# A spectral token-mixer kernel: modes loaded four blocks ahead in the last output, more tiles for the inverse transforms, and the sum x1 + lam y written for all blocks

## The chip, the cores and the metric

The kernel runs on one core of one Trainium2 chip. All data are float32. The metric is the device time of one launch, in microseconds (us); smaller is better. The profile is one execution of the same program with the hardware profiler on.

## The reference, cut to what matters

The input is 256 rows of 256 x 128 values. Layer 0 is a gated attention along the rows, added to its input; its result is called x1. Layer 1 sees x1 as 256 tokens (a token is an image of 256 x 128 pixels), lets the tokens attend to each other through a few Fourier modes of each image, and then mixes the tokens in groups of four with two Fourier layers. The diff touches only layer 1. Its end is this:

```python
attn = fno_layer(attn, p_wr, p_wi, p_bias, p_sw, p_sb, (H, W))
attn = instance_norm(attn + tokens, attn_norm_w, attn_norm_b)
attn = attn.reshape(b * (C // TOKEN_CODIM), TOKEN_CODIM, H, W)
h0 = instance_norm(attn, norm2_w, norm2_b)
h1 = fno_layer(h0, mix_wr[0], mix_wi[0], mix_bias[0], mix_sw[0], mix_sb[0], (H, W), norm=True, act=True)
h2 = fno_layer(h1, mix_wr[1], mix_wi[1], mix_bias[1], mix_sw[1], mix_sb[1], (H, W), norm=True)
out = instance_norm(h2, mon_w, mon_b) + attn        # and x1 is added to out by the caller

# fno_layer(x): skip = einsum(x, sw);  spec = irfft2(keep_low_modes(rfft2(x)) * w) + bias
#               y = (instance_norm(spec) if norm else spec) + skip;  gelu(y) if act
```

`instance_norm` takes mean and variance over the pixels of an image. The kernel writes the image before the mixer (attn + tokens, not yet normed) as y. The normed image is lam y plus a constant, so the final result is x1 + lam y + kap h2 + c0, with one lam, kap and c0 for each token.

## The kernel before, in words

**Halves, blocks, pixels.** The 256 tokens are cut into two halves of 128, `a` = 0 and 1; a token of the half is a partition. The 32768 pixels of an image are cut into 16 blocks of NB = 2048 pixels (b), each of two half blocks of HB = 1024 pixels (u or k in the code, 0 to 31). A tile of one half block is 128 x 1024 values, 512 KB; one of a block is 1 MB. All 16 blocks of one half stay in SBUF as `blocks` (`hb[b]` is one block), 16 MB; that is why other tiles are few.

**Fourier modes.** An image is kept as 32 x 16 modes. Turning modes into pixels takes two matmul steps. The first, `synth_modes` (lines 540 to 590), goes along the image's height: matmuls with `esyn` into four PSUM banks, four copies into a tile `gt` (128 x 2048 values, two by ACT and two by DVE, line 581), and four writes of a quarter each to a DRAM tensor `Gd` (line 586). It is called for one quarter of the modes at a time (`chunk` c = 0 to 3). The second, `image`, is done block by block: `load_modes` reads the modes of a block into a tile `gs` by four loads of 64 KB (lines 1199 and 1204), and 32 small matmuls (line 1182) add the image to PSUM. `skip` (line 1193) adds the channel product of four tokens to the same banks. Modes with a weight other than one are handled by a scaled copy `esyn0` of the first 32 rows of esyn, used for c = 0 and f = 0.

**Stages of layer 1.** They begin after some 1650 us; layer 0 is what comes before.
1. To about 1900 us: modes of x1, the attention between tokens (matrix `mpT`), and the modes of its result, written to `Gd0`.
2. `y_blocks(0)`, to about 2050 us: y of half 0. For each half block two tiles of x1 (one `xt` tile, line 997), 16 matmuls with mpT (line 1317), `image` from Gd0, four products by DVE (line 1327) into `blocks`, and statistics (line 1329). The first two blocks (b < NW = 2) are also written to the DRAM tensor `yd`. Before this stage a few small constants are loaded (ch4, sel4, s4, lines 1230 to 1255).
3. `y_blocks(1)`, half blocks 0 to 23, to about 2200 us: the same for half 1, all of it written to yd, woven with `first_modes(0)`, which computes the norm of y, the mixer's first product of modes (`mix_modes`) and the writes of `Gd1` of half 0.
4. `first_images(0)`, 2200 to 2345 us: for each block `skip` and `image` of Gd1 into `ups`, Gelu by ACT (line 1483) back into `blocks`, then, one block behind, 16 transposes (`htps`, line 1490), four copies `hT` (three by DVE, line 1502, one by ACT, line 1493), `skip` again for the statistics of the second layer (line 1510) and a forward transform (psA, yA, lines 1513 to 1516) into `Yd`. In the same loop, `load_w` and `add_w` (lines 1459 to 1470) make w = x1 + lam y for blocks 2 to 15: load x1 into half of an `xw` tile, lam y by ACT, the add by GpSimd (POOL), and a write to the DRAM tensor `wd`. This must come before Gelu overwrites y in `blocks`.
5. To about 2404 us: half blocks 24 to 31 of `y_blocks(1)`, woven with the start of `second_modes(0)`, which reads Yd back (tile `YT`, line 1534) and transforms it along the height (`f1ps`, line 1551).
6. 2404 to 2545 us: `mix_modes` of second_modes(0) (names z0) and of first_modes(1) (x1), their synth_modes (g20 into `Gd2` of half 0, g11 into `Gd1` of half 1), and blocks 0 to 4 of `output_0`. For blocks 0 and 1, `output_0` loads y and x1 and adds them itself (line 1637); for the others it loads w.
7. 2545 to 2716 us: `first_images(1)`, woven with blocks 5 to 15 of `output_0`.
8. 2716 to 2801 us: `second_modes(1)`, woven with `Output1.ahead`, which loads y and x of five half blocks (lines 1659 and 1661) and lets DVE make x1 + lam y in place (line 1666).
9. 2801 us to the end: `Output1.run`. For each block: `output` (lines 1594 to 1609), which does skip and image of Gd2 into `h2ps`, four ACT passes kap h2 + c0 (line 1602), two DVE adds to w (line 1608) and two writes by POOL's queue (line 1609); then the modes of block b + 2, DVE's add for further half blocks, and loads of y and x of half blocks 2b + 9 and 2b + 10.

**What sets the order.** From stage 2 on the order of instructions of each engine, SP included, is the order of the program text (`manual_schedule`). Python generators are woven by hand: `weave` advances a side generator when a running sum of written costs is positive. So SP issues its loads strictly one after another, and a load that waits for its tile holds all that follow. A tile's wait comes from its pool: `tile(tag, bufs=n)` gives the same memory again after n calls, and the first use then waits for the last use of the tile before. Loads go through SP; the writes of wd, yd, Yd, Gd1, Gd2 and of the result go through POOL's queue. DMA issues of SP and of ACT also take turns on eight semaphores: an issue waits until the DMA eight turns back has landed.

**Pools that matter here.** `xp` holds xt (3 tiles of 1 MB), gs (2) and yt (2). output_0 takes its tiles from the same tags until 2545 us. Output1 has two pools: `self.wp`, which lives from stage 8, and `more`, which opens at 2801 us. Before, half blocks k with k % 9 < 5 use `wp` (5 x tiles, 2 y tiles) and the others `more` (4 x tiles, 2 y tiles).

Of the kernel before, what the change touches and what calls it, by code (L numbers as in the profile page):

```python
# [10 lines left out]
FP = mybir.dt.float32  # L11
# [7 lines left out]
P = 128  # L19
# [493 lines left out]
def layer1(tc, I, C, ident, x1d, upool, U, stats2, mv2, out):  # L513
# [9 lines left out]
    with ExitStack() as ctx:  # L523
# [16 lines left out]
        def synth_modes(pool, psum, Z, T, Gd, tag, spare=None, turned=False, chunk=None, ptag="s", gbufs=2, queue=None):  # L540
# [4 lines left out]
            for c in range(4) if chunk is None else (chunk,):  # L545
                for part in range(1 if both else 2):
                    ps = [psum.tile([P, 512], FP, tag=ptag, name=f"{tag}gp_{c}_{part}_{f}") for f in range(4)]
                    gt = pool.tile([P, 4, 512], FP, tag="gt", name=f"{tag}gt_{c}_{part}", bufs=gbufs)
                    for ri in range(2) if both else (part,):
                        for jp in range(2):  # L550
                            k = 2 * ri + jp if both else jp
                            for i in range(2):
                                for f in range(4):
                                    q = slice(32 * f, 32 * f + 32)
                                    e = esyn0 if c == 0 and f == 0 else esyn
                                    trig = (1 - i if ri else 2 * i)
                                    if spare is not None and c == 0 and f == 0 and ri == 1:
                                        if i == 0:
                                            nc.tensor.matmul(
                                                ps[f][:, k * T : (k + 1) * T], e[0:32, 0, jp * P : (jp + 1) * P],  # L560
                                                spare, start=True, stop=True,
                                            )
                                    elif not turned:
                                        nc.tensor.matmul(
                                            ps[f][:, k * T : (k + 1) * T], e[q, trig, jp * P : (jp + 1) * P],
                                            Z[q, c, i, :], start=(i == 0), stop=(i == 1),
                                        )
                                    else:
                                        for jj in range(2):
# [7 lines left out]
                                                e[q, trig, j * 64 : (j + 1) * 64],  # L577
# [4 lines left out]
                    for ri in range(2) if both else (part,):  # L582
                        for jp in range(2):
                            k = 2 * ri + jp if both else jp
                            r0 = 16 * ri + 4 * c
                            (queue or nc.sync).dma_start(  # L586
# [58 lines left out]
        with tc.manual_schedule(engines=COMPUTE):  # L645
# [316 lines left out]
            esyn0 = late.tile([32, 3, H], FP, name="esyn0")  # L962
# [21 lines left out]
            nc.vector.tensor_scalar(esyn0, esyn[0:32], wsyn[0:32, 0:1], None, ALU.mult)  # L984
# [15 lines left out]
        xts = {(0, u): load_x1(0, u) for u in range(3)}  # L1000

# [90 lines left out]
        with tc.manual_schedule(engines=COMPUTE):  # L1092
# [46 lines left out]
            values(7, 1)  # L1139
            for c in range(4):  # L1140
                synth_modes(wp, psg0, Z, NT, Gd0, "g0", spare=m1, chunk=c)
                if c < 2:
                    values(7, c + 2)
# [21 lines left out]
        NW, NX = 2, 5  # L1165
# [59 lines left out]
        with tc.tile_pool(name="psb", bufs=4, space=PSUM) as psa, tc.tile_pool(name="spb", bufs=1) as spb:  # L1225
            same4 = load_const(spb, "same4")
            sel4 = load_const(spb, "sel4")

            ch4 = spb.tile([4, 6], FP, name="ch4")
            for i, src in enumerate(  # L1230
                (L("norm2_w"), L("norm2_b"), L("mix_sb")[0], L("mix_sb")[1], L("mon_w"), L("mon_b"))
            ):
                nc.sync.dma_start(ch4[:, i : i + 1], src.unsqueeze(1))
# [4 lines left out]
            an = sp.tile([P, 2], FP, name="an")  # L1238
            nc.sync.dma_start(an[:, 0:1], L("attn_norm_w").partition_broadcast(P))
            nc.sync.dma_start(an[:, 1:2], L("attn_norm_b").partition_broadcast(P))  # L1240

            blk = []
            for l in range(2):
                s4 = spb.tile([4, 4], FP, name=f"s4_{l}")
                with nc.allow_non_contiguous_dma(reason="16 elements"):
                    nc.sync.dma_start(s4, L("mix_sw")[l].rearrange("o i -> i o"))
                ps = psa.tile([P, 512], FP, tag="a", name=f"blkps_{l}")
                nc.tensor.matmul(ps[:, 0:4], sel4, s4, start=True, stop=True)
                r4 = spb.tile([P, 4], FP, name=f"r4_{l}")
                nc.vector.tensor_copy(r4, ps[:, 0:4])  # L1250
                bl = sp.tile([P, 32, 4], FP, name=f"blk_{l}")
                nc.vector.tensor_tensor(
                    bl, bc(r4, 1, 32), same4.rearrange("p (g o) -> p g o", o=4), ALU.mult
# [6 lines left out]
            nc.vector.tensor_scalar(hw0, wsyn[:, 1:2], 0.5, None, ALU.mult)  # L1260
# [660 lines left out]
```

## Time and profile before

Three runs gave 3015.53, 3019.59 and 3023.93 us; the median is 3019.59 us. The profiled execution has a span of 3018.5 us.

| engine | busy us | share of the span | instructions |
|---|---|---|---|
| PE (TensorE matmul) | 2621.3 | 87% | 28526 |
| PEld (weight load) | 1904.2 | 63% | 28526 |
| DVE (VectorE) | 2003.7 | 66% | 3223 |
| ACT (ScalarE) | 1467.7 | 49% | 2856 |
| POOL (GpSimd) | 1662.5 | 55% | 1310 |

Durations of single instructions that are needed below, in ns (mean of the group on the page or in an answer of the trace):

| line, engine | what | mean |
|---|---|---|
| L1327 DVE | y, one quarter of a half block, 128x256 | 418 |
| L1502 DVE / L1493 ACT | hT copy, 128x512 | 684 / 604 |
| L1510 DVE | statistics, 128x512 | 688 |
| L1466 ACT | lam y, 128x1024 | 1150 |
| L1469 POOL | x1 + lam y, 128x1024 | 2363 |
| L1666 DVE | x1 + lam y, 128x1024 | 1279 |
| L1608 DVE | w + blocks, 128x1024 | 1223 |
| L586 POOL | issue of one Gd write | 752 to 757 |
| L1609 POOL | issue of one result write | 535 |

How to read the page: busy time is the time in which an engine executes, and an engine that waits is not busy. A group's line gives the idle time just before its instructions and who ended it. The share of busy time is an average over stages with different limits, so the stage must be looked at by itself. "DMA" is the mean busy share of the core's 16 DMA engines, and "PEclk" the clock that TensorE was granted, as a share of full speed. SPq is the sequencer of SP, which issues loads; a wait there holds every later load.

### The profile page before, as it was taken

How to read it: one execution, taken by the hardware profiler on the slowest of the kernel's cores; microseconds unless marked ns; L12 is line 12 of the kernel's file. 1: busy time of each engine (PE TensorE's matmuls, PEld its weight loads, DVE VectorE, ACT ScalarE, POOL GpSimd, SP SyncE). 2: the span in 40 equal slices, each digit the busy share in tenths (PEclk: the TensorE clock that was granted, in tenths of full speed). 3: DMA queues.
4: the chain of work that ended last, by engine and by line, in shares of the span. 5: the costliest groups of instructions: out<-in, count | busy, mean ns of one | idle time of the engine just before them, and what ended most of it. 6: DMA issues, size and time to landing. Idle time of an engine off the chain costs nothing. (4 is left out here: it accounts for less than half of the span.)

```text
span 3018.5 us, 70144 instructions
## 1 busy us (share of the span) xinstructions
PE 2621.3 (87%) x28526; PEld 1904.2 (63%) x28526; DVE 2003.7 (66%) x3223; ACT 1467.7 (49%) x2856; POOL 1662.5 (55%) x1310
## 2 busy tenths in 40 slices
PE   6899999999999999999999899898998775886333
PEld 6677777777777777777776567686754543443111
DVE  7788888878888888888888447466555452563323
ACT  0477777777777777777776223000055013450212
POOL 0499999999999999999998002000257012111100
PEclk9999999999999999999999899999999887997555
DMA  9422222222222122222221012787878728974755
GB/s 364 154 66 65 71 66 66 65 73 66 64 72 66 66 65 72 66 64 72 65 66 47 19 50 78 255 274 267 309 259 299 258 77 292 323 264 150 260 213 210
DMA packets 226907, 430.02 MB, mean 142 GB/s; under 512 B 26070, under 2 KB 153513, under 8 KB 218520
## 3 DMA queue, kind: packets, MB, share of 16 engines
q1 hardware_dynamic: 200472, 333.24, 32.8%
q0 software_dynamic: 26112, 92.29, 8.6%
q8 instruction: 226, 3.70, 0.5%
q14 instruction: 97, 0.79, 0.1%
HBM read 290.17 MB, written 135.27 MB: 141 GB/s over the span
## 5 line engine op out<-in xcount | busy, mean ns | idle before, releaser
L299 POOL TENSOR_TENSOR e<-e,b1T 128x1024 f32<-128x1024 f32 x256 | 606.6, 2369 | 164.9 <-PE u L348 89.4
L303 POOL TENSOR_TENSOR es<-e 128x512 f32<-128x512 f32 x512 | 639.7, 1271 | 20.1
L281 ACT ACTIVATE sc<-sc,b2T 128x512 f32<-128x512 f32 x512 | 339.0, 662 | 365.0 <-PE sc L272 356.8
L323 DVE RECIPROCAL av<-av 128x256 f32<-128x256 f32 x256 | 452.3, 1767 | 27.2 <-DVE og L322 1.4
L281 ACT ACTIVATE e<-sc,b2T 128x512 f32<-128x512 f32 x512 | 348.6, 681 | 0.0
L294 DVE TENSOR_TENSOR e<-sc,b1T 128x1024 f32<-128x1024 f32 x256 | 311.0, 1215 | 0.0
L272 PE MATMUL sc<-qkT 32*128 32x256 f32 x4096 | 294.1, 401 | 1.3 <-DVE e L294 1.3
L311 PE MATMUL av<-e,v 128*32 128x256 f32 x4096 | 274.7, 385 | 0.5 <-POOL e L299 0.5
L1317 PE MATMUL yps<-xt,mpT 128*128 128x256 f32 x1024 | 245.9, 394 | 20.5 <-DMA xt<-x1d 10.4
L272 PEld LDWEIGHTS sc<-qkT 32*128 32x128 f32 x4096 | 185.6, 184 | 112.4 <-issue 97.8
L322 DVE SCALAR_TENSOR_TENSOR og<-gate,av 128x256 f32<-128x256 f32 x256 | 107.8, 421 | 190.6 <-PE av L316 190.6
L1317 PEld LDWEIGHTS yps<-xt,mpT 128*128 128x128 f32 x1024 | 195.1, 195 | 59.0 <-issue 10.9
L1182 PE MATMUL h2ps<-k_bsyn,gs 32*128 32x128 f32 x1024 | 65.0, 362 | 159.4 <-DMA gs<-Gd 159.4
L1602 ACT ACTIVATE blocks<-h2ps,col 128x512 f32<-128x512 f32 x128 | 89.2, 777 | 209.7 <-PE h2ps L1182 209.7
L327 POOL TENSOR_TENSOR x<-xt,bo 128x256 f32<-128x256 f32 x256 | 187.8, 734 | 0.0
L1182 PEld LDWEIGHTS h2ps<-k_bsyn,gs 32*128 32x128 f32 x1024 | 56.8, 253 | 201.1 <-DMA gs<-Gd 178.1
L246 PE MATMUL qk<-xnT,wT_wq 128*128 128x256 f32 x512 | 179.5, 432 | 1.7 <-ACT xnT L238 1.7
L1331 POOL DMA_DIRECT2D yd<-yt x32 | 17.3, 539 | 291.6 <-DVE yt L1327 291.6
L252 PEld LDWEIGHTS gv<-wT_wv,kvT 128*128 128x128 f32 x1024 | 155.0, 192 | 13.4
L316 PE MATMUL av<-es,ones 128*32 128x256 f32 x2048 | 157.5, 379 | 2.6 <-POOL es L303 2.5
L333 PE MATMUL wo<-wT_wo,og 128*128 128x128 f32 x1024 | 156.8, 276 | 2.7 <-DVE og L324 2.7
L348 PE MATMUL u<-adft,x 128*128 128x129 f32 x1024 | 156.4, 275 | 0.0
(532 smaller groups left out, 5347.3 us busy)
## 6 DMA issues: line engine op xcount, KB each, us to landing
xt<-x1d SPq DMA_DIRECT2D x128, 512.0 KB
xb<-in_x_dram SPq DMA_DIRECT2D x32, 1024.0 KB
xt<-in_x_dram SPq DMA_DIRECT2D x128, 256.0 KB
kt<-in_L_conv_kv_x_dram SPq DMA_DIRECT2D x128, 256.0 KB
x1d<-x SPq DMA_DIRECT2D x256, 128.0 KB
gs<-Gd SPq DMA_DIRECT2D x384, 64.0 KB
yd<-yt POOLq DMA_DIRECT2D x32, 512.0 KB, 5.5
y<-yd SPq DMA_DIRECT2D x16, 1024.0 KB
```

Source lines behind the costliest of these rows:

```text
L246: nc.tensor.matmul(ps[:, 0:256], wT["wq"], xnT, start=True, stop=True)
L272: nc.tensor.matmul(sc[h // 2][:, h % 2, c * 256 : (c + 1) * 256], qkT[p, 256 + c * P : 256 + (c + 1) * P], qkT[p, 0:256], start=True, stop ...
L281: nc.scalar.activation(r["e"][1][:, :, c, :] if hp else z, z, AF.Exp, bias=b2T[:, c, s : s + 1])
L294: nc.vector.tensor_tensor(r["e"][0].rearrange("p h c q -> p (h c q)"), r.pop("sc").rearrange("p h x -> p (h x)"), b1T[:, 0:2].rearrange("p ...
L299: nc.gpsimd.tensor_tensor(e1, e1, b1T[:, 2:4].rearrange("p h c q -> p (h c q)"), ALU.mult)
L303: nc.gpsimd.tensor_tensor(r["es"][hp], e[:, :, 0, :], e[:, :, 1, :], ALU.add)
L311: nc.tensor.matmul(ps[hd, 0:256], r["v"][:, c, hd], r["e"][h // 2][:, h % 2, c, :], start=(c == 0), stop=(c == 1),)
L316: nc.tensor.matmul(ps[32 * h : 32 * h + 32, 256:512], self.ones, r["es"][h // 2][:, h % 2, :], start=True, stop=True,)
L323: nc.vector.reciprocal(rd, rd)
L327: nc.gpsimd.tensor_tensor(r["x1"], r["x"], bc(self.bo, 1, 2), ALU.add)
L333: nc.tensor.matmul(ps[:, j * P : (j + 1) * P], r["og"][:, j * P : (j + 1) * P], wT["wo"], start=True, stop=True,)
L1317: nc.tensor.matmul(rows_of(ps[j]), mpT[:, sc, tt], by_turn(xt[:, sc])[:, j], start=(sc == 0), stop=False,)
```

## The change

The change has six parts.

1. **Output1**: `gs` gets four tiles (two in `wp`, two in `more`) and modes are loaded four blocks ahead. y has five tiles in turn (2 and 3), x has eight (5 and 3). Loads run for half blocks 2b + 8 and 2b + 9, and DVE's adds go up to half block 2b + 5.
2. **second_modes(1)**: two YT loads are issued at once, the others as tiles come free, and `ahead` starts only after the forward transform, with a cost of 0.4 for each step in place of 0.3.
3. **Inverse transforms**: `synth_modes` takes a list of pools for `gt`. g20 uses the three `xt` tiles, g11 takes its own tile and the xt tiles in turn. Of the four writes of a chunk, two are issued by POOL and two by ACT.
4. **w for all blocks**: `load_w` and `add_w` also run for blocks 0 and 1, so that output_0 has one form and y of half 0 is not written to yd. add_w of block b + 1 moves to just behind Gelu of block b. output_0 loads one block ahead, and its first load comes before the g11 chunks. In first_images(0) all four hT copies go to DVE.
5. **Small constants** (same4, sel4, ch4, an, s4) are loaded before the attention between tokens, and the two products with s4 become one.
6. **Weights of modes**: `esyn0` goes. The modes Z themselves are scaled in their first 32 rows (a separate tile Z0 in front of Gd0), and hw0 is divided by the weight again. `gs` in xp has three tiles in place of two.

The diff, cut to its core:

```diff
@@ synth_modes
-                    gt = pool.tile([P, 4, 512], FP, tag="gt", name=f"{tag}gt_{c}_{part}", bufs=gbufs)
+                    gp, gtag, gbufs = gts[c % len(gts)] if gts else (pool, "gt", 2)
+                    gt = gp.tile([P, 4, 512], FP, tag=gtag, name=f"{tag}gt_{c}_{part}", bufs=gbufs)
...
-                            (queue or nc.sync).dma_start(
+                            (queues or (nc.sync, nc.sync))[jp].dma_start(
@@ after xts, before the attention between tokens
+        par = _Held(tc.tile_pool(name="spb", bufs=1))
+        same4 = load_const(par.pool, "same4")
+        sel4 = load_const(par.pool, "sel4")
...
+            Z0 = sp.tile([32, 2, NT], FP, name="Z0")
+            nc.vector.tensor_scalar(Z0, Z[0:32, 0], wsyn[0:32, 0:1], None, ALU.mult)
@@ y_blocks
-                    gs[u // 2] = xp.tile([P, 4, P], FP, tag="gs", name=f"gs_{a}_{u}")
+                    gs[u // 2] = xp.tile([P, 4, P], FP, tag="gs", name=f"gs_{a}_{u}", bufs=3)
...
-                if a or b < NW:
+                if a:
                     nc.gpsimd.dma_start(ydv[:, a, u * HB : (u + 1) * HB], yt)
@@ mix_modes
+            nc.vector.tensor_scalar(Z[0:32, 0], Z[0:32, 0], wsyn[0:32, 0:1], None, ALU.mult)
@@ first_images
             load(0)
+            if a == 0:
+                load_w(0)
+                add_w(0)
...
-                    if a == 0 and b + 1 >= NW:
+                    if a == 0:
                         load_w(b + 1)
...
                         nc.scalar.activation(by_turn(hb[b])[:, j], rows_of(ps[j]), AF.Gelu)
+                    if a == 0 and b < 15:
+                        add_w(b + 1)
...
-                            nc.scalar.copy(t, ps)
+                            (nc.scalar.copy if a else nc.vector.tensor_copy)(t, ps)
...
-                if a == 0 and NW <= b + 1 < 16:
-                    add_w(b + 1)
@@ second_modes
             load(0)
             yield 6.0
+            if gbufs > 1:
+                load(1)
             for c in range(4):
-                if gbufs > 1 and c < 3:
-                    load(c + 1)
...
-                if gbufs == 1 and c < 3:
-                    load(c + 1)
+                if c + gbufs < 4:
+                    load(c + gbufs)
                     yield 4.0
@@ output_0
-                if b < NW:
-                    got[b] = [xp.tile([P, 2, HB], FP, tag="xt", name=f"xy_{b}_{s}", bufs=3) for s in range(2)]
...
+            load(0)
+            yield
             for b in range(16):
                 if b not in got:
                     load(b)
+                if b < 15 and pools[3]:
+                    load(b + 1)
@@ Output1.load
-                more = k % (NX + 4) >= NX
-                wp = self.more if more else self.wp
-                y = wp.tile([P, HB], FP, tag="yo", name=f"y4_{k}", bufs=2)
+                old = k < 5 or k % 5 < 2
+                y = (self.wp if old else self.more).tile(
+                    [P, HB], FP, tag="yo", name=f"y4_{k}", bufs=2 if old else 3
+                )
                 nc.sync.dma_start(y, ydv[:, 1, px])
-                x = wp.tile([P, HB], FP, tag="xo", name=f"x4_{k}", bufs=4 if more else NX)
+                x = (self.wp if k % 8 < 5 else self.more).tile(
+                    [P, HB], FP, tag="xo", name=f"x4_{k}", bufs=5 if k % 8 < 5 else 3
+                )
@@ Output1.run
-                    gs[b] = self.wp.tile([P, 4, P], FP, tag="gs", name=f"gs3_1_{b}")
+                    gs[b] = (self.wp if b % 4 < 2 else self.more).tile(
+                        [P, 4, P], FP, tag="gs", name=f"gs3_1_{b}", bufs=2
+                    )
...
-                for k in range(NX, NX + 4):
+                for k in (5, 6, 7):
                     self.load(k)
+                modes(2)
+                modes(3)
                 for b in range(16):
                     run(output(1, b, gs.pop(b), [self.w.pop(2 * b), self.w.pop(2 * b + 1)], psk))
-                    if b < 14:
-                        modes(b + 2)
+                    if b < 12:
+                        modes(b + 4)
                     for k in sorted(self.ld):
-                        if k < 2 * b + 4 or k < NX + 2 * b:
+                        if k <= 2 * b + 5:
                             self.add(k)
-                    for k in (2 * b + NX + 4, 2 * b + NX + 5):
+                    for k in (2 * b + 8, 2 * b + 9):
                         if k < 32:
                             self.load(k)
@@ the weaving
-                    m0 = second_modes(0, wp, tiles(wp), bq)
+                    m0 = second_modes(0, wp, tiles(wp), bq, [(xp, "xt", 3)])
...
+                    m1 = first_modes(
+                        1, wp, Tiles(F=(xp, "yt", 2), f=(xp, "yt", 2), m=(xp, "gs", 3)), br,
+                        [(wp, "gt", 1), (xp, "xt", 3)],
+                    )
...
                     o0 = output_0(pools, bq)
+                    next(o0)
...
-                    m1 = second_modes(1, wp, tiles(wp), Banks(psq, "q"), gbufs=2)
-                    weave((0.3 for _ in m1), o1.ahead())
+                    m1 = second_modes(1, wp, tiles(wp), Banks(psq, "q"), [(wp, "gt", 2)], gbufs=2)
+                    run(iter(lambda: next(m1), None))
+                    weave((0.4 for _ in m1), o1.ahead())
```

## The prediction, made before the changed kernel ran

> **What bounds the kernel now.** The slices of the page show two kernels in one. Up to about 1650 us (layer 0) PE is busy throughout and DMA at two tenths; the diff does not touch that. From 1900 us on DMA moves 200 to 300 GB/s and PE, its clock and DMA all sag at the end. So I cut this second part into its stages and asked for busy times of each (columns: stretch; length; PE, PEld, DVE, ACT, POOL busy with counts; granted clock; DMA share; GB/s):
>
> ```profile
> 2182.00:2192.00 10.00, 9.01 (x67) 7.21 (x66) 5.66 (x13) 0.00 (x0) 1.18 (x3) 1.00 1.03 376
> 2202.00:2345.00 143.00, 122.64 (x1896) 62.37 (x1892) 74.79 (x120) 80.81 (x124) 94.98 (x74) 1.00 0.84 282
> 2404.00:2447.00 43.00, 33.54 (x80) 14.89 (x80) 30.79 (x69) 3.35 (x7) 0.53 (x1) 0.88 0.19 67
> 2447.00:2482.00 35.00, 19.64 (x300) 16.21 (x300) 11.51 (x26) 5.75 (x12) 11.96 (x16) 0.78 0.42 116
> 2482.00:2545.00 63.00, 32.35 (x832) 21.78 (x832) 24.23 (x38) 19.71 (x30) 17.50 (x26) 0.69 0.78 273
> 2545.00:2716.00 171.00, 147.27 (x2624) 79.51 (x2624) 94.19 (x134) 81.08 (x140) 23.34 (x37) 0.92 0.88 297
> 2716.00:2748.00 32.00, 12.31 (x256) 9.66 (x256) 3.72 (x7) 0.38 (x1) 0.75 (x1) 0.66 0.64 222
> 2748.00:2776.00 28.00, 21.16 (x54) 9.11 (x58) 17.73 (x33) 2.95 (x5) 0.00 (x0) 0.80 0.21 75
> 2776.00:2801.00 25.00, 14.09 (x306) 11.86 (x306) 9.28 (x24) 4.50 (x9) 11.92 (x16) 0.70 0.61 170
> 2801.00:3018.00 217.00, 67.95 (x992) 40.58 (x992) 70.06 (x59) 44.57 (x64) 17.13 (x32) 0.56 0.64 228
> ```
>
> The first row is a ceiling: ten microseconds of plain large transfers, share 1.03 at 376 GB/s. Against it, three stretches stand out as limited by nothing but waits: 2404 to 2482 (mixer modes, DMA 0.19 and 0.42), 2716 to 2801 (the last modes), and the last output, 217 us long, with DMA at 0.64, PE at 0.56 clock, DVE a third busy. First images (2202 to 2345) and the woven stage (2545 to 2716) are near the DMA limit at 0.84 and 0.88.
>
> The last output is the largest, so I took its waits, SP's own queue first (waiter, releaser: total us, times, longest), then PE's:
>
> ```profile
> SPq L1659 <- DVE x L1666: 121.9, 11, 13.8
> SPq L1661 <- DMA x<-x1d: 9.0, 8, 1.6
> ```
>
> ```profile
> PE h2ps L1182 <- DMA gs<-Gd: 142.4, 14, 14.4
> ```
>
> PE waits 142 us for modes, yet SP, which has to issue their loads, stands 122 us behind DVE's line 1666. One period in order of time shows why:
>
> ```profile
> 2875.22 2.48 DVE L1666 SCALAR_TENSOR_TENSOR x<-y,col,x 128x1024 f32<-128x1024 f32 x2
> 2877.72 0.32 SPq L1659 DMA_DIRECT2D y<-yd  x1
> 2878.67 1.77 SPq L1199 DMA_DIRECT2D gs<-Gd  x4
> 2883.23 2.59 PE L1182 MATMUL h2ps<-k_bsyn,gs 32*128 32x128 f32 x32 [10.79 <-DMA gs<-Gd]
> 2885.45 2.79 ACT L1602 ACTIVATE blocks<-h2ps,col 128x512 f32<-128x512 f32 x4 [12.54 <-PE h2ps L1182]
> 2888.26 2.36 DVE L1608 TENSOR_TENSOR x<-x,blocks 128x1024 f32<-128x1024 f32 x2 [10.57 <-ACT blocks L1602]
> ```
>
> DVE finishes x1 + lam y at 2877.70; only then is a buffer for the next y free; SP issues y, x and, behind them in its queue, the modes of the next block at 2878.67; PE has them at 2883.23, ACT 2.2 us later, DVE at 2888.26, and its adds release SP again. It is a ring of 13 to 16 us a block, with one block in flight.
>
> The middle has the same shape, with one gt tile and one DMA round trip a chunk; before the y stage PE waits for eight small constants, issued at 1902 to 1905; and in first images the queue of xw tiles shows on POOL and, through ACT's order, on PE:
>
> ```profile
> ACT g20gt L581 <- DMA Gd<-g20gt: 21.3, 3, 8.1
> PE h2ps L1182 <- DMA gs<-Gd: 16.1, 3, 12.1
> ```
>
> ```profile
> PE chps L1235 <- DMA ch<-in_L_conv_mon_b_dram: 10.3, 1, 10.3
> ```
>
> ```profile
> POOL xw L1469 <- DMA xw<-x1d: 16.8, 14, 2.5
> PE sps L1193 <- ACT hT L1493: 15.7, 12, 2.5
> ```
>
> **What the Trainium skill says.** *Perfetto Trace Analysis*, section Optimization Strategy: the same gap repeating on the engine that should be saturated can mean that tiles are short (buffer count). The trace agrees: 14 waits for gs, up to 14.4 us each, behind a y tile with two buffers. *DMA: Bandwidth & Descriptors*, section Rules for kernel authors: issuing from SP, ACT and GpSimd does not add bandwidth, all use the same 16 engines; it saves only issue time. Here issue time is worth having: POOL needs 0.75 us for each Gd write, 3.0 us a chunk. The same page, section Specifications, puts the HBM limit of a core near 358 GB/s; the trace's 376 is somewhat above. *TensorE: Matmul & The Clock Gate*, part 1: an idle PE runs at half clock. The output stage agrees with clock 0.56 and 420 ns a matmul of line 1182, against about 302 ns for the same shape in the images.
>
> **The change part by part.**
>
> (1) *Last output.* Modes get four tiles and are loaded four blocks ahead; y goes from a reuse distance of two to five, x from nine tiles to eight; adds reach one half block further. In the new order SP issues modes(b+4), y and x of 2b+8, y and x of 2b+9 at block b. y(2b+9) needs the add of 2b+4, done in this or the previous block, instead of one two blocks later. What remains is x(2b+8), which needs the write of half block 2b to land (issue to landing 3.2 us in the median). Modes are behind that on SP, but are needed four blocks later. The remaining loop: write of block b, 3 to 5 us; load, 5 to 8; DVE's adds at block b+2, 2.5; output of block b+3. That is 11 to 16 us for three blocks, about 5 a block. DVE needs 2.36 + 2.48 = 4.8 us a block, PE 2.6 + 2.0 = 4.6, ACT 2.8. So DMA becomes the limit: 27 y, 27 x and 32 writes of 0.524 MB and 64 modes loads of 0.066 MB are 49.3 MB; the DMA view put their work at 41.3 + 21.8 = 63% of 220 us, 139 us. At the 0.88 that the woven stage reaches this takes 158 us; 2 us for the first modes and 6 for the last write and the end make 166. Before 217: **-51 us**. At 0.95 it would be 154 (-63); at a period of 11.5 us a block, if the loop holds it, 192 (-25).
>
> (2) *Second modes of half 1.* The four YT loads (1 MB each) go ahead of y and x. Before, YT was in at 2744, 25 us after the last Yd write, with 2 MB of y and x between; 2 MB at some 250 GB/s are 8 us, so **-9** (bounds -4, -11). One more add of 1.28 us falls into the product chain: **+1**. The Gd writes of g21 go half to ACT: POOL's chunk falls from 3.0 to 1.5 us; three chunks stood in line, and an ACT issue costs between SP's 0.35 and POOL's 0.75 us, I take 0.5, beside POOL's: **-5** (0 to -8). ACT has nothing queued behind but the next chunk's copies.
>
> (3) *Middle, 2447 to 2545.* g20 takes three xt tiles, g11 alternates gt and xt. The three waits of 8 us for g20's write go; a chunk then costs PE 2.5 and copies 1.3 us, with the product steps of the other half between, about 4 us instead of 9. x1's norm, which stood on ACT behind those copies, moves up with it: g11 starts 11 us sooner (2482 to 2471). Then four chunks with an output block each. Before, 11 us a block, with 12.1 us in one wait for gs loaded too late; now loads are one block ahead and blocks 0 and 1 read one w (1 MB) in place of y and x (2 MB). A block moves w 1.05, out 1.05, gs 0.26, Gd1 0.26 MB, 2.6 MB; at 310 GB/s 8.4 us, say 8.5: 4 x 2.5 = 10. Together **-20**, lower bound -5 if the writes only queue elsewhere, upper -32. ACT's write issue can wait for a DMA whose semaphore it takes over, with the evacuation of h2ps behind it; the outputs wait on the same loads, so I cost that at nothing.
>
> (4) *First images of half 0.* hT's fourth copy moves from ACT (0.60) to DVE (0.68): DVE then has 8 x 0.67 = 5.4 us of a block of 9; the 15.7 us of PE waits for it shrink. But the period grew from 7.5 us (first four blocks) to 9.2 once three xw tiles turned over: add 2.36, write about 4.5, load about 4.5, issues and turns 1.5 to 2.5, 13 to 14 us a tile, two of three tiles a block, hence about 9. The change keeps three tiles and adds blocks 0 and 1 to the turning: 2 x 1.7 = +3.4. Of the hT waits I give back a third, -5. Four yd writes go from the y stage of half 0; its PE is at 100%, so they were hidden. Sum **-2**, from -12 to +15.
>
> (5) *Constants early.* The 10.3 us wait goes; the first image then waits for gs, issued at 1895 to 1898, about 1903 instead of 1914.5, and that stage is PE-bound, so it carries: **-9** (-5 to -11).
>
> (6) *Z scaled instead of esyn.* One scaling of 32 rows before Gd0 and one in each of four mode stages, 0.2 to 0.5 us each, on the path: **+1.5**. par, hw0, s4 and three gs tiles: nothing, beside DMA or PE-bound work.
>
> Sum: -51 -9 +1 -5 -20 -2 -9 +1.5 = -93.5; 3019.6 - 93.5 = **2926 us**.
>
> **The rivals.**
> A, better: writes and loads saturate (0.95, -63) and the middle gives -32: 2926 - 12 - 12 = 2902. For it: share 1.03 in the first row. Against: 0.88 in the mixed stages.
> B, the wait moves to x: SP blocks on the out write of the block just issued, one tile fewer than before, period 11.5: 2926 + 26 = 2952. For it: SP's x rows already wait 9.0 us. Against: three blocks of slack.
> C, the middle gives 5 only and first images turn at 9.8 us (157 for 143, +14, instead of -2): 2926 + 15 + 16 = 2957. For it: POOL's 95 us busy of 143 and DMA at 0.84.
> D, slower: the modes were not the releaser and the output ring stays at 13 us (0), first images go to 11 us a block (176, +33), the middle 0; with -9, -13 and +1.5 left: 3019.6 + 12.5 = 3032. Against: the period above shows SP's order directly.
>
> **How the numbers follow.** Forecast 0.52, A 0.17, B 0.16, C 0.09, D 0.04, no change 0.02. The range from 2888 to 2966 holds the forecast's spread, A, B and C, and leaves out D, no change and the tails of A and C. Faster 0.94, same 0.02, slower 0.04.
>
> **What would show it.** In the changed profile: the last stage some 165 us long, DMA above 0.85, PE's wait for gs below 30 us, SP's for DVE's add near zero and some for out_dram; no wait of g20gt for Gd; no chps wait; YT in within 17 us of the last Yd write; first images still near 9 us a block. Wrong if the output stage keeps a period above 12 us, if DMA stays near 0.65 there with SP behind out_dram, or if ACT's Gd issues hold up h2ps.

## The result, and the profile after

The changed kernel takes 2914.72 us (median of 4 runs, 2908.14 to 2927.72) against 3019.27 us for the kernel before beside it: ratio 0.9658, 95% interval 0.9622 to 0.9694. Run again in the last group of experiments it took 2922.72 us against 3018.32: 0.9672 (0.9655 to 0.9690). The prediction was 2926 us.

Busy times of five stages of the changed kernel, cut at the same events as in the prediction: first images of half 0; g20; g11 with its output blocks; the woven stage; the last output (columns: stretch; length; PE, PEld, DVE, ACT, POOL busy with counts; granted clock; DMA share; GB/s):

```profile
2194.00:2324.00 130.00, 115.00 (x1792) 57.99 (x1786) 72.75 (x118) 68.88 (x103) 96.24 (x72) 0.99 0.86 288
2444.00:2468.00 24.00, 17.89 (x300) 14.74 (x304) 10.95 (x27) 5.85 (x12) 5.99 (x8) 0.77 0.74 220
2468.00:2533.00 65.00, 31.18 (x848) 20.65 (x856) 18.51 (x30) 19.59 (x30) 11.50 (x18) 0.74 0.77 256
2533.00:2694.00 161.00, 139.74 (x2480) 75.61 (x2459) 85.92 (x120) 77.25 (x132) 21.78 (x36) 0.89 0.89 305
2785.00:2926.00 141.00, 77.66 (x992) 48.27 (x992) 70.93 (x59) 44.44 (x64) 17.08 (x32) 0.58 0.94 351
```

The last row is where most of the gain lies: the same 992 matmuls, 59 DVE and 64 ACT instructions in 141 us instead of 217, with DMA at 0.94 instead of 0.64. In the middle of that stage it is higher still:

```profile
2800.00:2825.00 25.00, 16.38 (x259) 9.66 (x259) 10.83 (x9) 11.03 (x16) 2.13 (x4) 0.70 1.03 395
2850.00:2875.00 25.00, 16.96 (x192) 10.45 (x192) 14.28 (x12) 8.32 (x12) 3.19 (x6) 0.57 1.03 386
```

What SP's queue waits for in the last output of the changed kernel (waiter, releaser: total us, times, longest), to be held against 121.9 us behind DVE before:

```profile
SPq L1663 <- DMA x<-x1d: 32.0, 22, 2.5
SPq L1659 <- DMA y<-yd: 24.0, 21, 1.7
SPq L1659 <- DVE x L1668: 0.5, 2, 0.4
```

And what the engines wait for there:

```profile
DVE x L1668 <- DMA x<-x1d: 49.9, 24, 3.0
PE h2ps L1200 <- DMA gs<-Gd: 42.3, 12, 6.0
```

The plug is gone: SP's wait for DVE's add fell from 121.9 to 0.5 us, and PE's wait for modes from 142.4 to 42.3. SP, DVE and PE now wait a little, 1 to 6 us at a time, for a transfer in flight. One period in order of time (start, duration, instruction, idle before it and its releaser):

```profile
2860.26 3.73 PE L1200 MATMUL h2ps<-k_bsyn,gs 32*128 32x128 f32 x32 [3.75 <-DMA gs<-Gd]
2860.28 1.91 SPq L1217 DMA_DIRECT2D gs<-Gd  x4
2860.86 2.35 DVE L1621 TENSOR_TENSOR x<-x,blocks 128x1024 f32<-128x1024 f32 x2
2863.62 2.78 ACT L1615 ACTIVATE blocks<-h2ps,col 128x512 f32<-128x512 f32 x4 [6.50 <-PE h2ps L1200]
2868.84 3.78 PE L1200 MATMUL h2ps<-k_bsyn,gs 32*128 32x128 f32 x32 [2.91 <-DMA gs<-Gd]
2869.00 1.82 SPq L1217 DMA_DIRECT2D gs<-Gd  x4
2869.49 2.35 DVE L1621 TENSOR_TENSOR x<-x,blocks 128x1024 f32<-128x1024 f32 x2
```

From image to image this period takes 8.6 us. The one that the prediction shows took 15.5, from the line below to 2883.23:

```profile
2867.69 2.81 PE L1182 MATMUL h2ps<-k_bsyn,gs 32*128 32x128 f32 x32 [13.51 <-DMA gs<-Gd]
```

By the start times of the image matmuls, the mean from block 6 to block 15 (counted from 0) is 8.9 us a block, where it was 13.5; single periods went from 5 to 18 us before and go from 8.3 to 9.5 now.

"Four blocks ahead" holds only in the program's text. Counted from the start of the stage, the gs load at 2860.28 is the one of block 11, and the matmuls of block 11 begin at 2868.84: SP asks for the modes one block ahead, 8.6 us before their use. Before, it asked 4.6 us before it (2878.67 to 2883.23), and only after DVE's work on the block in between. SP is late because its loads take turns on eight semaphores, and in this stage a block has just eight loads, four of gs, two of y, two of x. In the part of the trace read for this (2838 to 2875 us), each gs load for which it shows what ended its wait waited for the gs load eight turns back. SP's waits for y and x transfers, 24.0 and 32.0 us above, fit the same turns. So SP has about one block's loads under way at a time, whatever the text allows.

To see the smaller parts, I read the start times of the first and last matmuls of named tiles. One profile is not enough for a few microseconds, so the last column takes all profiles of the changed kernel and of experiments whose code in that stage is the changed kernel's (9 to 13 of them; the kernel before has one):

| stage, us | before | changed | mean of all (range) | difference |
|---|---|---|---|---|
| start to first image of first_images(0) | 2199.9 | 2194.4 | 2191.7 | -8.2 |
| first_images(0), first to last `ups` | 124.0 | 129.5 | 131.6 (128.8 to 134.3) | +7.6 |
| then to the last z0 sum | 115.0 | 111.8 | 110.2 (106.5 to 114.2) | -4.8 |
| middle, to the first `ups` of half 1 | 107.6 | 97.1 | 96.5 (94.6 to 97.9) | -11.1 |
| woven stage, first to last `ups` | 158.0 | 160.7 | 158.1 (154.5 to 162.5) | 0 |
| then to the last g21 product | 82.9 | 80.3 | 76.7 (73.7 to 80.3) | -6.2 |
| then to the end | 231.1 | 151.9 | 153.1 (150.9 to 155.1) | -78.0 |

The sum of the differences is -101 us; nearly four fifths lie in the last output.

### The profile page after: what moved, and what is told of

The parts are those of the page before. It is cut to its first block, busy times and chain, and to the rows that moved or that the text cites. A ratio compares the mean times of both kernels' runs of the same rounds, so it can differ in the third digit from the quotient of the medians.

```text
span 2925.7 us, 70150 instructions
## 1 busy us (share of the span) xinstructions
PE 2638.9 (90%) x28524; PEld 1916.9 (66%) x28524; DVE 2007.8 (69%) x3239; ACT 1460.9 (50%) x2844; POOL 1647.0 (56%) x1282
## 5 line engine op out<-in xcount | busy, mean ns | idle before, releaser
L1324 PE MATMUL yps<-xt,mpT 128*128 128x256 f32 x1024 | 244.5, 393 | 21.9 <-DVE yt L1334 11.1
L1324 PEld LDWEIGHTS yps<-xt,mpT 128*128 128x128 f32 x1024 | 194.1, 194 | 60.2 <-DVE yt L1334 14.2
L311 PEld LDWEIGHTS av<-e,v 128*32 128x32 f32 x4096 | 107.0, 109 | 76.1 <-POOL e L299 1.0
L252 PE MATMUL gv<-wT_wv,kvT 128*128 128x128 f32 x1024 | 156.0, 275 | 0.0
```

What stands on the lines that cost most here:

```text
L252: nc.tensor.matmul(ps[:, 256 + c * P : 256 + (c + 1) * P], kvT[:, c * P : (c + 1) * P], wT["wv"], start=True, stop=True,)
L311: nc.tensor.matmul(ps[hd, 0:256], r["v"][:, c, hd], r["e"][h // 2][:, h % 2, c, :], start=(c == 0), stop=(c == 1),)
L1324: nc.tensor.matmul(rows_of(ps[j]), mpT[:, sc, tt], by_turn(xt[:, sc])[:, j], start=(sc == 0), stop=False,)
```

## The experiments

### Which part has the gain, and what limits the last output now

**The last output put back.** In the changed kernel, the whole class `Output1` as it was, tiles too:

```diff
-                    if b < 12:
-                        modes(b + 4)
+                    if b < 14:
+                        modes(b + 2)
...
-                        if k <= 2 * b + 5:
+                        if k < 2 * b + 4 or k < 5 + 2 * b:
                             self.add(k)
-                    for k in (2 * b + 8, 2 * b + 9):
+                    for k in (2 * b + 5 + 4, 2 * b + 5 + 5):
```

> The changed kernel with the last output's loads, tiles and order put back as they were (two modes ahead, two y tiles per pool, x loads nine half blocks ahead). Theory (nearly all of the gain is the last output, 76 us of 105 by the marks of the two traces): about 2991 us, the last output back at 210 to 220 us. Rival (the last output is short because it begins in a better state, with other parts of the change having the gain): 2915 to 2945 us.

Measured: 2998.55 us, ratio 0.9926 (0.9896 to 0.9955), where the full change has 0.9658. The last stage is back, plug and all. Its wait on SP and its busy row:

```profile
SPq L1658 <- DVE x L1665: 121.9, 10, 13.7
```

```profile
2774.00:2997.00 223.00, 68.96 (x1008) 40.33 (x992) 71.45 (x69) 44.55 (x64) 17.53 (x33) 0.55 0.64 226
```

All other parts together give 19 us (3017.66 - 2998.55; 14 to 31 by the interval); the last output gives the rest.

**Which half of that edit.** The prediction named two things: the y tile that SP stood in front of, and the modes that lay behind it. Two kernels keep one each. Modes two blocks ahead in the text (the first four lines of the diff above), with the new x and y tiles and the new place of the adds and loads:

> The changed kernel with new x and y tiles, but the modes of the last output asked for two blocks ahead instead of four. Theory A (the queue behind the waiting y load set the pace, so the three more y tiles and the new order give the gain): 2915 to 2930 us, PE's waits for the modes a little longer. Theory B (the modes' distance of four blocks gives it): 2970 to 2990 us, PE's waits for gs back over 100 us.

Modes four ahead in the text, with the old y and x tiles and the old place of the adds and loads (the last lines of that diff, and the loads' tiles):

> The changed kernel with modes four blocks ahead, but the old x and y tiles (two y tiles in each pool in blocks of five and four, x loads nine half blocks ahead, the old place of the adds). Theory A (the wait of the y load for the add was the plug of the queue): 2970 to 2990 us, SP again waits for DVE's add before y loads. Theory B (modes' distance): 2915 to 2935 us, with the wait for DVE's add still there but with nothing starved behind it.

Measured: 2922.29 us (0.9677, 0.9651 to 0.9703) and 2920.31 us (0.9680, 0.9662 to 0.9698). Both have nearly all of the gain; neither theory's "back to 2970" came. SP's main waits and the busy row of the stage, modes two ahead:

```profile
SPq L1663 <- DMA out_dram<-x: 38.0, 14, 6.0
```

```profile
2770.00:2919.00 149.00, 71.44 (x992) 43.45 (x992) 70.49 (x59) 44.53 (x64) 17.08 (x32) 0.58 0.92 335
```

and with the old y tiles:

```profile
SPq L1658 <- DVE x L1665: 46.0, 14, 7.6
```

```profile
2770.00:2920.00 150.00, 76.29 (x1024) 45.83 (x992) 72.41 (x70) 44.64 (x65) 18.07 (x34) 0.59 0.92 338
```

With the modes two ahead, SP stands 38 us behind the output's writes (rival B of the prediction), and that costs nearly nothing. With the old y tiles SP still stands 46 us behind DVE's add, and that costs nearly nothing either. Here, too, the modes go out about one block ahead of their use. With the modes two ahead no add holds them: the load of block 10 goes out as the matmuls of block 9 begin (2855.98). Load and matmuls of block 10:

```profile
2856.15 1.85 SPq L1217 DMA_DIRECT2D gs<-Gd  x4
2865.75 2.65 PE L1200 MATMUL h2ps<-k_bsyn,gs 32*128 32x128 f32 x32 [4.86 <-DMA gs<-Gd]
```

and of block 11, with the old y tiles:

```profile
2862.67 1.77 SPq L1217 DMA_DIRECT2D gs<-Gd  x4
2868.35 3.82 PE L1200 MATMUL h2ps<-k_bsyn,gs 32*128 32x128 f32 x32 [1.87 <-DMA gs<-Gd]
```

With the old y tiles the load still stands behind an add, but, being two blocks later in the text, no longer behind DVE's work on the block just before its own: it goes out 1.9 us after the matmuls of block 10 begin (2860.76), where before it went out 11 us after those of the block ahead (2867.69 to 2878.67). So the ring of the kernel before needed both: a plug in the queue, and something urgent behind it. Cutting it in either place lets the stage run into the next limit, which looks the same in all three kernels (DMA at 0.92 to 0.94). By the marks their last stages are 158.1 and 155.5 us against 153.1: by these single profiles the second cut is worth some 2 to 5 us, and the run times do not show it.

**Is that limit the DMA engines?** The x loads left out, y taken in their place:

```diff
-                nc.sync.dma_start(x, x1v[:, 1, px])
...
-                nc.vector.scalar_tensor_tensor(x, y, halves[1].col[:, 3:4], x, ALU.mult, ALU.add)
+                nc.vector.scalar_tensor_tensor(x, y, halves[1].col[:, 3:4], y, ALU.mult, ALU.add)
```

> The changed kernel with the 32 loads of x1 in the last output left out (y is taken in its place, so the output is not the reference's); 16.8 of 54.5 MB less to move in that stage. Theory (the last output is now bound by the DMA engines, share 1.03): its period falls from 9 us toward 6.2 us a block by bytes, so 2870 to 2885 us, or where another engine sets in, at the latest 7.5 us a block and 2893 us. Rival (it is bound by the chain of gs, PE, ACT, DVE and the tiles, and the DMA share is only an effect): 2908 to 2920 us.

Measured: 2873.01 us (0.9529, 0.9512 to 0.9546); the stage falls by 38.9 us (153.1 to 114.2). Only 27 of the 32 x loads lie inside the stage, 14.2 of its 49.5 MB; at the 386 GB/s of the changed kernel they take 36.7 us. The rate stays where it was although 31% of the traffic of a block is gone:

```profile
2800.00:2850.00 50.00, 38.48 (x550) 21.02 (x546) 40.40 (x34) 23.84 (x35) 9.60 (x18) 0.60 1.03 394
```

34 DVE instructions, four to a block, make a period of 5.9 us. So PE, ACT, DVE and the order can do a block in 5.9 us, and the 8.9 of the changed kernel look like the bytes. One rival has to be weighed: the edit also leaves six loads in a block instead of eight, which eases SP's eight turns. If the turns alone set the pace, the period would fall to 6/8 of 8.9, 6.7 us; by the bytes it would fall to 6.2 (2.36 of 3.41 MB). From block 6 to block 15 it is 6.0 us, with the share still at 1.03, which speaks for the bytes. A kernel with more turns was not run.

### First images of half 0: what costs 7 us

**One copy back to ACT:**

```diff
-                            (nc.scalar.copy if a else nc.vector.tensor_copy)(t, ps)
+                            nc.scalar.copy(t, ps)
```

> The changed kernel with one of four copies of a block of the first images (hT, turn 0, batch half 0) given back to ACT. The stage from the first to the last image of first_images(0) takes 129.5 us after the change and 124.0 us before it. Theory (ACT's order is what costs: lam times y waits for the ring of xw and yA lies behind it; the copy on ACT adds to this): the stage gets longer, 130 to 136 us. Rival (DVE carries too much with all four copies, and this is what costs the 5.5 us): 122 to 126 us. In time: 2915 to 2925 us against 2908 to 2914 us.

Measured: 2923.43 us (0.9688, 0.9662 to 0.9715), the stage 134.6 us, where the changed kernel has 128.8 to 134.3. The copy on DVE is not what costs; it may save some 3 us, which one profile can't settle.

**The next block's lam y and add back at the end of a turn:**

```diff
-                    if a == 0 and b < 15:
-                        add_w(b + 1)
...
+                if a == 0 and b < 15:
+                    add_w(b + 1)
                 yield 1
```

> The changed kernel with lam times y and the add of the next block back at the end of a block's turn, behind yA, for all 16 blocks. Theory (yA queues on ACT behind lam times y, which waits for the ring of xw): the waits of PE's transposes for ACT's yA (8.8 us) vanish and the stage shrinks from 129.5 to 122 to 126 us, the whole to 2908 to 2914 us. Rival (the place makes no difference, since the ring of xw is what is short: two more blocks go through it): 128 to 131 us, 2913 to 2922 us.

Measured: 2918.93 us (0.9671, 0.9645 to 0.9697), the stage 131.7 us. PE's wait of 8.0 us for ACT's yA is gone, and one of 9.6 us for modes took its place. The theory that ACT's order held the stage up falls.

**The first two blocks apart, as before**, so that 14 blocks instead of 16 go through the ring of three xw tiles:

```diff
-                    if a == 0:
+                    if a == 0 and b > 0:
                         load_w(b + 1)
...
+                if b < 2:
+                    t = [wp.tile([P, 2, HB], FP, tag="xt", name=f"xy_{b}_{s}", bufs=3) for s in range(2)]
```

> The changed kernel with the first two blocks handled as before: their y written out, read back with x1 in the middle, added by DVE; 14 blocks through the ring of xw instead of 16. Theory (two blocks more in the first images cost about 5 us there, and save about as much DVE and DMA time in the middle): first_images(0) down from 129.5 to about 124 us, but the middle (last sum of z for layer 0 to the first image of first_images(1), 97 us after the change) up by 3 to 8 us: 2912 to 2922 us, no difference that the end shows. Rival (the edit brings the middle its gain): middle up by 10 us or more, 2922 to 2935 us.

Measured: 2912.87 us (0.9641, 0.9611 to 0.9672); the stage 124.7 us, 7 less than with 16 blocks and as before the change (124.0). The middle is 98.4 instead of 96.5. So two more blocks in the ring cost about 3.5 us each and give back some 2 us in the middle. This part of the change, "x1 + lam y for all blocks", costs some microseconds; the run times alone, whose intervals overlap, would not show it.

### The middle and the last modes

**Modes ahead of w on SP.** In the changed kernel `load(b)` of the first output asks for w, then for the modes:

```diff
+                gs = gp.tile([P, 4, P], FP, tag="gs", name=f"gs3_0_{b}", bufs=3 if gp is xp else 2)
+                load_modes(gs, halves[0].Gd2, b)
                 t = wp.tile([P, NB], FP, tag="xt", name=f"w_{b}", bufs=bufs)
                 nc.sync.dma_start(t, wd[:, b * NB : (b + 1) * NB])
-                gs = gp.tile([P, 4, P], FP, tag="gs", name=f"gs3_0_{b}", bufs=3 if gp is xp else 2)
-                load_modes(gs, halves[0].Gd2, b)
```

> The changed kernel with the modes of a block of the first output asked for ahead of its w tile. In the changed kernel, PE waits 7 us each in two of the middle's blocks for modes that lie on SP behind a w load that waits for the xt tile. Theory (the order on SP is what keeps the middle from its forecast gain): these two waits go, the middle is 8 to 14 us shorter, 2902 to 2910 us. Rival (the w tile itself comes late and DVE's add or the next block takes the wait, as the xt tiles come free only with the writes of the output): below 3 us, 2912 to 2918 us.

Measured: 2903.55 us (0.9613, 0.9581 to 0.9644). The middle falls from 96.5 to 87.1 us and the woven stage, where the same loads go on, from 158.1 to 150.5. (The changed kernel did not run beside this one; the two kernels above that are as fast as it, one copy back to ACT and the add at the end, did, with 2923.43 and 2918.93 us.) In the changed kernel PE waited some 7 us in each of two output blocks of the middle, and SP in front of w for an output's write to leave the tile:

```profile
PE h2ps L1200 <- DMA gs<-Gd: 14.3, 3, 7.2
```

```profile
SPq L1631 <- DMA out_dram<-w: 23.4, 2, 12.5
```

With the modes first, h2ps has no wait for gs in the middle. It is the fault of the last output over again, in a stage whose order on SP the change left as it was: a load that waits for its tile, and in the queue behind it one that is needed sooner.

**All writes of modes on POOL's queue:**

```diff
-                            queues=(nc.gpsimd, nc.scalar))
+                            queues=(nc.gpsimd, nc.gpsimd))
```

> The changed kernel with all writes of modes back on POOL's queue, none on ACT's. The stage from the last sum of z to the last g21 product took 19.6 us before, 18.8 to 20.3 us in seven profiles of the changed kernel and its variants; z0's last sum to the first g11 product 43.6 before, 30.5 to 32.1 after. Theory (the second queue gives nothing that the end sees): both marks within 1 us of that, 2914 to 2922 us. Rival (the second queue is what brings the middle's 12 us): z0's last sum to the first g11 product back at 36 to 44 us, 2922 to 2934 us.

Measured: 2923.89 us (0.9677, 0.9656 to 0.9698), beside 2922.72 us for the changed kernel on the same chip; g21 20.0 us, z0 to g11 31.1 us. The second queue gives nothing that the end sees.

**One gt tile for g20 and for g11:**

```diff
-                    m0 = second_modes(0, wp, tiles(wp), bq, [(xp, "xt", 3)])
+                    m0 = second_modes(0, wp, tiles(wp), bq, [(wp, "gt", 1)])
...
-                        [(wp, "gt", 1), (xp, "xt", 3)],
+                        [(wp, "gt", 1)],
```

> The changed kernel with the middle's two syntheses (g20, g11) using one gt tile again, as before the change. Theory (the wait of the copies for the write out of the one tile is what made the middle long: 10.6 us less in g20 and its successor): z0's last sum to the first g11 product up from 31 to 38 to 44 us, the last g11 product to follow by as much, 2924 to 2932 us. Rival (the second queue and other edits do it): 2914 to 2922 us.

Measured: 2922.24 us (0.9688, 0.9669 to 0.9707). The copies wait again for the one tile's write (the waits of the middle):

```profile
ACT g20gt L584 <- DMA Gd<-g20gt: 16.4, 3, 6.6
DVE g20gt L584 <- DMA Gd<-g20gt: 13.7, 3, 6.5
```

and g11 starts 40.5 us after z0's last sum instead of 31.3. But the whole middle is longer by only 4.3 us (100.8 to 96.5), and the run time doesn't show it. So of the 9 us won ahead of g11 half is lost behind it, in the waits for the modes of the first output shown above: with one gt tile, h2ps has no wait for gs there.

**The two that gave something, together, and the changed kernel beside them:**

> The changed kernel with two edits that gave something alone: the modes ahead of the w tile in the first output, and the first two blocks handled as before (y written out, x1 and y read back in the middle). If they add up (9.5 us in the middle and 7 in the woven stage by the first, 7 us in the first images less 2 in the middle by the second): 2892 to 2900 us. If the middle's x and y loads of the two blocks stand in front of the modes again or what one saves the other has already: 2900 to 2908 us.

> The changed kernel as it is, beside the other three on the same chip, so that they can be compared with it as well as with the kernel before: 2912 to 2922 us, the stages within 2 us of the means so far (first images 131, middle 96, woven 157, second_modes(1) up to its first sum 36, last output 153).

Measured: both edits 2896.84 us, 0.9599 (0.9573 to 0.9625); the changed kernel 2922.72 us, 0.9672 (0.9655 to 0.9690). This version is faster than both kernels, than the changed one by 26 us. The total adds up (17 us by the marks of the first edit, 5 by those of the second), but not stage by stage: first images 121.8 us, woven stage 146.4, both better than with one edit, and the middle 93.1, where 87.1 + 1.9 = 89.0 was to be expected. There SP waits again for the tiles and loads of the two blocks (6.7 us for out_dram<-xy, 3.6 for xy<-yd).

## Why the prediction was right, and where it was off

*Last output* (forecast -51, measured -78): the ring was read rightly, the size is wrong. The view of one period gave the ring, and the changed trace shows it cut: 121.9 us behind DVE became 0.5, the limit became DMA. The bytes were right too (49.3 MB worked out, 49.46 in the trace). The term that was mis-sized is the rate: "at the 0.88 that the woven stage reaches" was taken as a ceiling for mixed loads and writes, for 158 us. But the woven stage is not limited by DMA alone (the exchange of two statements took 7.6 us from it); the last output ran at 1.03 and 382 to 395 GB/s for 100 us, as the first row of the prediction's table already did for 10, at 376 GB/s. Taking 1.03 there (139 us of DMA work) would have given 135 + 8 = 143 us, and 141 came (with a little help: in the changed trace the same work is 0.94 x 141 = 133 us). Even rival A's 0.95 was too low.

Three more points of this step were only half right. The prediction did not ask whether y's distance and the modes' distance were both needed; each alone is enough. That the modes "are needed four blocks later" is so in the text alone: SP, held by its eight turns, asks for them one block before their use. The turns had no term in this step; what they cost beyond the DMA limit is open. And PE's wait for gs was to be below 30 us; it was 42.3, in twelve waits of at most 6.0. SP's forecast wait of x for the output's writes does not appear in the changed kernel, though it does with the modes two ahead (38.0 us).

*Second modes of half 1* (-9 for YT, +1 for an add, -5 for ACT's queue: -13; measured -6.2). From the last image to the last f1 product the time fell by 5.7 us (42.1 to 36.4 in the mean), so the YT order is right and its size two thirds of the forecast. The sign that was asked for, YT in within 17 us of the last Yd write, did not come: the last f1 group starts 22.7 us after that write's issue (27.6 before), and it still waits 3.2 us for its YT (2.9 before), while y and x loads are already under way. ACT's queue gave nothing (g21 takes 20.0 us without it and 18.8 to 20.4 with it): the copies wait for a gt tile's write to land (ACT 6.0 us and DVE 3.3, before 8.7 and 5.5), not for POOL to issue it, and the number of gt tiles here (two) is as before.

*Middle* (-20, measured -11.1). Its first half held: g11 12 us sooner, forecast 11. Its second half, "now loads are one block ahead", four blocks times 2.5 us, gave nothing (64.0 to 65.0 us from the first g11 product to the first image of half 1). SP issues w ahead of the modes, w waits for an xt tile, and the modes arrive late; with the order turned, the middle is 87.1 us, -20.5. I had looked at the distance of the loads and not at what stands ahead of them in the queue, although this was what I had found in the last output.

*First images* (-2, measured +7.6, inside the bounds of -12 to +15). The cost of two more blocks in the ring was taken as 2 x 1.7 us; it is 2 x 3.5. The 5 us credited to the copy on DVE are some 3 by one profile: PE's wait for ACT's hT (13.2 us before) went, and one for ACT's yA (8.0 us) took its place. With 14 blocks in the ring the stage is as long as before the change, 124.7 to 124.0 us, so the other edits in it cancel.

*Constants* (-9): the wait is gone, PE's first small product now waits 0.8 us for DVE, and the stage up to the first images is 8.2 us shorter in the mean. The place is right: from the last g0 product to the first image matmul of y it took 25.9 us before and takes 12.8 in all 13 profiles. That is 13 us; g0's products (26.1 to 28.3 us in the mean) and the y stages (285.4 to 287.2) take back 4. *Z scaled* (+1.5) is one edit among those that may have lengthened g0's products; no run separates it.

The stage between first images and z0 gave 4.8 us that I had not forecast; before, PE waited 10.4 us there for xt tiles and now 7.1, but no experiment was made on it.

That the total, -93.5 against some -101, is so near is luck in good part: the forecast gave 27 us too little to the last output and 25 too much to the second modes, the middle and the first images together, and knew nothing of the 5 us of that other stage.

## What to carry to other kernels

When a queue of loads stalls, look for a pair: a load that waits for its tile, and behind it one that is needed sooner. Here cutting either was enough, and then the next limit decided, so work out the bytes at the highest rate that the trace shows anywhere, not at that of a stage bound by something else. A load that the text places four blocks ahead need not be issued four blocks ahead: read in the trace when it goes out and when its data are used. After moving loads ahead, read the order of the queue again for the same pair; here it was left in another stage, and there the exchange of two statements was worth 17 us by the marks, nearly as much as all the smaller parts of the change together.

## What was not expected of the hardware

Mixed traffic, two parts read and one part written, ran from 2800 to 2900 us at share 1.03 and 387 GB/s (382 to 395 in pieces of 25 us). That is above the 358 GB/s that the Trainium skill, *DMA: Bandwidth & Descriptors*, section Specifications, gives as a core's HBM limit, worked out there as half of what one stack gives to two cores; here the kernel runs on one core, and the measurement decides. At this load an output write of 0.5 MB took 7.8 us from issue to landing in the median, where it took 3.2 us in the last output of the kernel before, at share 0.64. So a tile's time in flight was no constant of the transfer's size, and a ring of tiles sized by the first figure may be too short at the second (no run here tests that alone).
